# Affine weights of a modulated linear layer loaded in two transfers, and a one-column copy placed early on ScalarE

## The chip, the cores and the metric

The kernel runs on one core of one Trainium2 chip. The metric is the device time of one execution in microseconds (us), given as the median of several runs. A profiled execution gives the busy times, the waits and the transfers; its "span" runs from the first to the last instruction that the profiler saw.

## The reference, cut to what matters

The input x has 8 batches of 1024 tokens with 512 channels. A conditioned linear layer is computed first, and a mixture-of-experts feed-forward layer on its result; the sum with x is returned.

```python
styles = w @ (affine_w / 16).T + affine_b          # 8 x 512, w = cond_512 (8 x 256)
ws = weight[None] * styles[:, None, :]
dcoefs = rsqrt(sum(ws * ws, axis=2) + 1e-8)
y = einsum('blc,oc->blo', x * styles[:, None, :], weight) * dcoefs[:, None, :]
y = clip(y + bias, -256, 256)
...
x + shared_ffn(y) + routed_ffn(y)                  # 64 experts, 8 chosen per token
```

The change touches only what comes before the first products of the einsum: the loading of `affine_w`, the styles, and the scaling of x by them.

## The kernel before, in words

The 8192 tokens are handled as 16 tiles of 512. For about the first 241 us the conditioned layer is computed tile by tile (line L319), with the router's logits (L344); the shared experts follow (L124, L1083), up to about 1311 us, while the routing table is built; then the routed experts (L564, L584) run to the end. Every fp32 operand of a big product is split into a rounded high part and a remainder (`wh` and `wl` for the weights, `xh` and `xl` for the scaled tokens), and three products are summed for each: high by high, low by high, high by low.

The start of the kernel, which the change touches, goes like this. SyncE (SP) loads the affine weights `af` in one transfer of 512 KB (L225), then the four 256 KB row blocks of the linear layer's weights `wr` (L240). ScalarE (ACT) starts transfers too: the condition `cd` (L227), the vectors `vc` (L229, biases) and the four 256 KB blocks `xr` of the first token tile (L241), and only then computes. SP goes on with `rr`, `cs`, `ebb` (L243 to L245), eight stores of zeros (L293, L294) and the next token tile (L236).

`styles()` (L255 to L271) has TensorE multiply `af` by `cd` in 8 fp32 matmuls of 8 columns (L260; the profile counts each as two passes, 16 in all) into two PSUM tiles `ps`: the first holds the 128 channels of block 0, the second those of blocks 1 to 3. Then for each block k of 128 channels: ACT copies `wr` to `wh` (L262), VectorE (DVE) makes the styles `sty` of block 0, or of blocks 1 to 3, from `ps` (L266), ACT scales `xr` to `xh` (L302) and DVE makes `xl` (L303), DVE makes `wl` (L268; the profile shows the helper's line L72), and GpSimd (POOL) squares `wr` into `w2` (L271; the profile calls it `w`). TensorE multiplies by block k as soon as the parts are there (L319: per output block `xh` by `wh`, `xl` by `wh`, `xh` by `wl`). The squares are used later by the demodulation matmuls (L277, tile `psm`), which stand before block 3's products.

The order on PE, ACT and DVE is the one in which the calls are written (`manual_schedule`); the order on SP and POOL is the scheduler's. Each engine works off its list in order, so a waiting instruction holds up all behind it on its engine. The transfers that SP and ACT start share eight completion semaphores, taken in turn in the order of the code; a transfer isn't started before the one eight places ahead of it, which has the same semaphore, has landed. ScalarE needs a function table before its first computing instruction; the compiler puts the load of the table straight in front of it. Tiles of the pool `xa` that share a tag share two buffers: `af` and `wr` lie in those of `yf` (the layer's output), and the tag `lt` belongs to the router's logits.

Of the kernel before, what the change touches and what calls it, by code (L numbers as in the profile page):

```python
# [11 lines left out]
F32 = mybir.dt.float32  # L12
# [9 lines left out]
P = 128  # L22
B, L, C = 8, 1024, 512
# [43 lines left out]
def body(ctx, tc, xT, x, condT, wT, vecs, affT, rwT, ebias, wexp, shgu, shdn, cst, out):  # L67
    nc = tc.nc
    V, S, PE, GP, SP = nc.vector, nc.scalar, nc.tensor, nc.gpsimd, nc.sync

    def sub(o, a, b):
        V.tensor_tensor(o, a, b, ALU.subtract)  # L72
# [145 lines left out]
    with ExitStack() as actx:  # L218
        wa = actx.enter_context(tc.tile_pool(name="wa", bufs=1, reuse_waits="tile"))
        xa = actx.enter_context(tc.tile_pool(name="xa", bufs=2, reuse_waits="tile"))  # L220
        psa = actx.enter_context(tc.tile_pool(name="psa", bufs=1, space=PSUM, reuse_waits="tile"))

        xs, xhl, st = {}, {}, {}
        af = xa.tile([P, 2, C], F32, name="af", tag="yf")
        SP.dma_start(af, affT.rearrange("(k p) o -> p k o", p=P))  # L225
        cd = wa.tile([P, 2, B], F32, name="cd")
        S.dma_start(cd, condT.rearrange("(k p) b -> p k b", p=P))  # L227
        vc = wa.tile([P, 2, KC], F32, name="vc")
# [10 lines left out]
        for k in range(KC):  # L239
            SP.dma_start(wr[:, k], wv[k])  # L240
            S.dma_start(xs[0][k], xT[0, :, k * TT:(k + 1) * TT])  # L241
        rr = wa.tile([P, KC, E], F32, name="rr")
        SP.dma_start(rr, rwT.rearrange("(k p) e -> p k e", p=P))  # L243
        SP.dma_start(cs, cst)
# [10 lines left out]
        def styles():  # L255

            ps0 = [psa.tile([P, n, B], F32, name="ps0", tag="py", bufs=3) for n in (1, KC - 1)]
            for m in range(KC):
                for k in range(2):
                    PE.matmul(ps0[m > 0][:, max(m - 1, 0)], lhsT=af[:, k, m * P:(m + 1) * P], rhs=cd[:, k], start=k == 0, stop=k == 1)  # L260
            for k in range(KC):
                S.copy(wh[:, k], wr[:, k])  # L262
                if k < 2:
                    ks = slice(0, 1) if k == 0 else slice(1, KC)
                    n = ks.stop - ks.start
                    V.scalar_tensor_tensor(sty[:, ks], ps0[k], 1.0 / 16.0, vc[:, 1, ks].unsqueeze(2).to_broadcast([P, n, B]), ALU.mult, ALU.add)  # L266
                split_x(0, k)
                sub(wl[:, k], wr[:, k], wh[:, k].bitcast(F32))  # L268
                if k == 1:
                    V.tensor_tensor(sty2, sty, sty, ALU.mult)  # L270
                GP.tensor_tensor(w2[:, k], wr[:, k], wr[:, k], ALU.mult)  # L271
# [24 lines left out]
        def split_x(j, k):  # L296
            b = j * TT // L
            if k == 0:
                xhl[j] = ([], [])
            h = xa.tile([P, TT], F32R, name="xh", bufs=6)  # L300
            l = xa.tile([P, TT], F32R, name="xl", bufs=6)
            S.activation(h, xs[j][k], AF.Copy, scale=sty[:, k, b:b + 1])  # L302
            V.scalar_tensor_tensor(l, xs[j][k], sty[:, k, b:b + 1], h.bitcast(F32), ALU.mult, ALU.subtract)  # L303
            xhl[j][0].append(h)
            xhl[j][1].append(l)
# [111 lines left out]

        with tc.manual_schedule(engines={ET.PE, ET.Activation, ET.DVE}):
            styles()

            load_x(1)
# [823 lines left out]
```

## Time and profile before

| what | value |
|---|---|
| time, median of 3 runs | 3718.44 us (3717.13 to 3718.55) |
| the profiled execution's own time | 3718.36 us |
| its span | 3716.6 us |
| TensorE: busy, share of the span | 3684.8 us, 99% |
| VectorE, ScalarE, GpSimd busy | 2005.9, 1736.5, 2086.7 us |
| first TensorE instruction starts | 5.01 us |
| granted TensorE clock, mean | 0.996 |

Busy shares are means over the whole span. What a change at the start does must be read from the first 30 us: the timeline there (start, duration, engine, line, operation, tiles, count, and in brackets how long the engine was idle before and what ended that), the chain of waits followed back from the end, and the engine's busy time in chosen stretches with the clock that TensorE was granted and the rate of the transfers. "PEld" is TensorE's weight load, "SPq" and "ACTq" are transfers being started by SP and ACT.

### The profile page before, as it was taken

The page shows a single profiled execution, that of the slowest core. Times are in us where ns is not written, and L with a number is a line of the kernel's source. Part 1 is how long each engine was busy: PE and PEld are TensorE (multiplying, and loading weights), DVE is VectorE, ACT ScalarE, POOL GpSimd, SP SyncE. Part 2 cuts the span into 40 slices and gives each one's busy share as a digit, 9 for nine tenths or more (in the row PEclk, how much of TensorE's full clock was granted, in tenths as well). Part 3 has the DMA queues.
Part 4 walks back from the last instruction along what each step waited for, and adds up shares of the span by engine and source line. Part 5 has one row for each costly group of instructions (what it writes and reads, how often), then busy time and mean ns, then how long its engine had stood idle before and what let it go on. Part 6 is the DMA issues. An engine that isn't in the chain of part 4 may idle for free.

```text
span 3716.6 us, 49611 instructions
## 1 busy us (share of the span) xinstructions
PE 3684.8 (99%) x17819; PEld 3053.1 (82%) x17819; DVE 2005.9 (54%) x3196; ACT 1736.5 (47%) x2676; POOL 2086.7 (56%) x1597
## 2 busy tenths in 40 slices
PE   8999999999999999999999999999999999999997
PEld 7778888888888888888888888888888888888886
DVE  6766666666653255555455554555555555555553
ACT  6652111111111155555555555555555555555554
POOL 0001666666666055666666656666656666656563
PEclk9999999999999999999999999999999999999999
DMA  8862212122122277776777777788787777877664
GB/s 257 239 176 71 64 36 57 46 47 58 38 56 53 94 177 156 149 148 156 148 144 157 166 181 163 170 178 194 145 176 143 167 146 177 171 151 132 115 118 66
DMA packets 238739, 491.23 MB, mean 132 GB/s; under 512 B 43074, under 2 KB 75858, under 8 KB 230803
## 3 DMA queue, kind: packets, MB, share of 16 engines
q0 software_dynamic: 135840, 280.28, 40.6%
q1 hardware_dynamic: 101651, 206.63, 18.4%
q8 instruction: 142, 2.33, 0.3%
q14 instruction: 114, 0.93, 0.1%
q10 hardware_dynamic: 992, 1.06, 0.1%
HBM read 443.20 MB, written 195.63 MB: 172 GB/s over the span
## 4 chain that ended last, share of the span: by engine, by line
PE 98%; DVE 1%; DMA 0%; ACT 0%; issue 0%; POOL 0%; SPq 0%; ACTq 0%; DVEq 0%; POOLq 0%
PE pg L564 38%; PE po L584 20%; PE gu L124 19%; PE po L1083 9%; PE pt L541 4%; PE py L319 4%; PE pg L573 1%; PE plt L344 1%; DMA xr<-in_xT 0%; PE psm L367 0%; ACT yf L325 0%; DVE yl L72 0%; PE pg L578 0%; DVE yt L356 0%; PE ps L1004 0%
## 5 line engine op out<-in xcount | busy, mean ns | idle before, releaser
L591 POOL DMA_INDIRECT out<-oc,tokw x532 | 915.9, 1722 | 663.4 <-ACT oc L588 203.5
L1053 POOL DMA_INDIRECT tab_d<-tokw,ad x512 | 567.8, 1109 | 500.3 <-DVE h L136 220.1
L564 PE MATMUL pg<-xh,gh 128*128 128x512 f32 (+1 forms) x2176 | 838.7, 385 | 0.0
L564 PE MATMUL pg<-xh,gl 128*128 128x512 f32 (+1 forms) x2176 | 823.5, 378 | 0.0
L564 PE MATMUL pg<-xl,gh 128*128 128x512 f32 (+1 forms) x2176 | 821.6, 378 | 0.0
L537 POOL DMA_INDIRECT xg<-y_d,tokw x532 | 589.2, 1107 | 328.7 <-PE pt L541 141.5
L72 DVE TENSOR_TENSOR xl<-pt,xh 128x512 fp32r<-128x512 f32 x532 | 352.6, 687 | 406.6 <-ACT xh L544 405.7
L588 ACT ACTIVATE oc<-po,tokw 128x512 f32<-128x512 f32 x532 | 367.6, 691 | 316.4 <-PE po L584 279.6
L564 PEld LDWEIGHTS pg<-xh,gl 128*128 128x128 f32 x2176 | 409.1, 188 | 78.6
L564 PEld LDWEIGHTS pg<-xl,gh 128*128 128x128 f32 x2176 | 409.5, 188 | 71.8
L564 PEld LDWEIGHTS pg<-xh,gh 128*128 128x128 f32 x2176 | 408.7, 188 | 71.0
L584 PE MATMUL po<-dh,hh 128*128 128x512 f32 x1064 | 428.1, 402 | 0.8 <-ACT hh L713 0.8
L711 DVE TENSOR_TENSOR hf<-hf,pg 128x512 f32<-128x512 f32 x240 | 164.9, 687 | 488.0 <-PE pg L564 488.0
L584 PE MATMUL po<-dh,hl 128*128 128x512 f32 x1064 | 418.2, 393 | 0.0
L584 PE MATMUL po<-dl,hh 128*128 128x512 f32 x1064 | 415.3, 390 | 0.0
L72 DVE TENSOR_TENSOR gl<-wg,gh 128x1024 fp32r<-128x1024 f32 x312 | 376.2, 1222 | 52.0 <-ACT gh L552 51.4
L124 PE MATMUL gu<-yl,guh 128*128 128x512 f32 x1024 | 400.2, 391 | 0.0
L124 PE MATMUL gu<-yh,guh 128*128 128x512 f32 x1024 | 399.7, 390 | 0.0
L124 PE MATMUL gu<-yh,gul 128*128 128x512 f32 x1024 | 398.1, 389 | 0.0
L544 ACT CAST xh<-pt 128x512 fp32r<-128x512 f32 x532 | 296.9, 587 | 188.8 <-PE pt L541 133.1
L552 ACT CAST gh<-wg 128x1024 fp32r<-128x1024 f32 x312 | 323.9, 1048 | 27.1 <-PE pg L564 27.1
L708 ACT ACTIVATE hf<-pg 128x512 f32<-128x512 f32 x240 | 144.0, 600 | 294.3 <-PE pg L564 289.3
(246 smaller groups left out, 5206.5 us busy)
## 6 DMA issues: line engine op xcount, KB each, us to landing
wg<-in_wexp SPq DMA_DIRECT2D x156, 1024.0 KB
wd<-in_wexp SPq DMA_DIRECT2D x156, 512.0 KB
y_d<-yt SPq DMA_DIRECT2D x64, 256.0 KB
xn<-in_x SPq DMA_DIRECT2D x64, 256.0 KB
out<-xn SPq DMA_DIRECT2D x64, 256.0 KB
xr<-in_xT SPq DMA_DIRECT2D x60, 256.0 KB
yT_d<-yf SPq DMA_DIRECT2D x60, 256.0 KB
yr<-yT_d SPq DMA_DIRECT2D x60, 256.0 KB
```

The lines of the kernel that those rows point to most:

```text
L72: V.tensor_tensor(o, a, b, ALU.subtract)
L124: i_ = PE.matmul(p_, lhsT=w_[:, q * KC + k], rhs=y_[k], start=n == 0, stop=n == 3 * KC - 1)
L537: queued(GP.indirect_dma_start(xg[g % RXG].bitcast(F32), None, y_d, IOA(slot_tok[:, u.block + s:u.block + s + 1], 0)))
L544: S.copy(xh[u.xq][:, :, s * P:(s + 1) * P], pt_of(g).bitcast(F32))
L552: S.copy(a[u.q][:, sl], (wg, wg, wd)[c][u.kind][:, sl])
L564: PE.matmul(out, lhsT=w_[u.q][:, c:c + P], rhs=x_[u.xq][:, k, :w], start=n == 0, stop=n == 3 * KC - 1)
L584: PE.matmul(po[d % 2], lhsT=h_[u.q][:, k, s * P:(s + 1) * P], rhs=w_[u.q][:, k * C:(k + 1) * C], start=n == 0, stop=n == 5)
L588: S.mul(oc[d % ROC], po[d % 2], slot_w[:, u.block + s:u.block + s + 1])
L591: i_ = queued(GP.indirect_dma_start(out, IOA(slot_tok[:, u.block + s:u.block + s + 1], 0), oc[d % ROC], None, compute_op=ALU.add))
L711: mu = add((i, "mu", m), "DVE", 0.69, 0.15, t0, lambda b=b, f=f: V.tensor_tensor(hf[f % 3], hf[f % 3], pg[(b + 1) % 4], ALU.mult), si, p)
L1053: i_ = GP.indirect_dma_start(places, IOA(ad, 0), tw, None)
L1083: PE.matmul(acc[j][s], lhsT=h_[:, ts], rhs=w_[c], start=c == 0 and n == 0, stop=c == HC - 1 and n == 2)
```

## The change

The affine weights come in two transfers: `af[0]` with the first 128 channels (128 KB) stays first on SP, and `af[1]` with the other 384 (384 KB) is started behind the first block of `wr`. `af[0]` takes a buffer of the tag `lt`. A tile `nil` of one column is set to zero on DVE, and ACT copies it onto itself behind its third transfer (`cd`, `vc`, `xr` block 0), ahead of the other three blocks of `xr`; being ACT's first computing instruction, the copy now has the function table's load in front of it. The matmuls of `styles()` read `af[0]` for block 0 and `af[1]` for blocks 1 to 3.

```diff
@@ -221,8 +221,12 @@
         xs, xhl, st = {}, {}, {}
-        af = xa.tile([P, 2, C], F32, name="af", tag="yf")
-        SP.dma_start(af, affT.rearrange("(k p) o -> p k o", p=P))
+
+        nil = wa.tile([P, 1], F32, name="nil")
+        V.memset(nil, 0.0)
+        af = [xa.tile([P, 2, P], F32, name="af0", tag="lt"), xa.tile([P, 2, C - P], F32, name="af", tag="yf")]
+        afv = affT.rearrange("(k p) o -> p k o", p=P)
+        SP.dma_start(af[0], afv[:, :, :P])
         cd = wa.tile([P, 2, B], F32, name="cd")
@@ -239,6 +243,9 @@
         for k in range(KC):
             SP.dma_start(wr[:, k], wv[k])
             S.dma_start(xs[0][k], xT[0, :, k * TT:(k + 1) * TT])
+            if k == 0:
+                SP.dma_start(af[1], afv[:, :, P:])
+                S.copy(nil, nil)
@@ -257,7 +264,7 @@
             for m in range(KC):
                 for k in range(2):
-                    PE.matmul(ps0[m > 0][:, max(m - 1, 0)], lhsT=af[:, k, m * P:(m + 1) * P], rhs=cd[:, k], start=k == 0, stop=k == 1)
+                    PE.matmul(ps0[m > 0][:, max(m - 1, 0)], lhsT=af[m > 0][:, k, max(m - 1, 0) * P:max(m, 1) * P], rhs=cd[:, k], start=k == 0, stop=k == 1)
```

## The prediction

> **What bounds the kernel now.** The page comes first: it says which engine carries the span.
>
> ```profile
> span 3716.6 us, 49611 instructions
> PE 3684.8 (99%) x17819; PEld 3053.1 (82%) x17819; DVE 2005.9 (54%) x3196; ACT 1736.5 (47%) x2676; POOL 2086.7 (56%) x1597
> ```
>
> TensorE is idle for 31.8 us in all. The busy times by stretch (columns: stretch, length, busy time and instructions of PE, PEld, DVE, ACT, POOL, granted clock, transfer share, GB/s) tell where:
>
> ```profile
> 0.00:8.60 8.60, 3.59 (x17) 3.59 (x17) 1.68 (x4) 3.13 (x4) 4.24 (x12) 1.00 0.75 237
> 8.60:26.60 18.00, 18.00 (x81) 14.87 (x82) 11.09 (x21) 8.50 (x13) 2.93 (x2) 0.91 0.96 333
> ...
> 3700.00:3716.60 16.60, 0.00 (x0) 0.00 (x0) 0.00 (x0) 0.00 (x0) 2.48 (x2) 0.55 0.35 50
> ```
>
> 5.0 us go before TensorE's first instruction, 16.6 behind its last; in between it is nearly never idle, so a shift at the start goes through to the end. All that the change can move lies before 8.6 us. The chain of waits there:
>
> ```profile
> 0.75 4.21 DMA cd<-in_condT
> 4.97 0.04 issue
> 5.01 3.58 PE ps L260 x16
> 8.59 3.84 PE py L319 x9
> ```
>
> Transfers until 5.01, then the 16 passes of the styles, then the layer. The timeline of the same stretch shows that a second path ends at the same moment:
>
> ```profile
> 5.16 1.28 ACT L262 ACT_TABLE_LOAD   x1 [5.16 <-DMA af<-in_affT]
> 5.54 2.04 POOL L271 TENSOR_TENSOR w<-wr 128x512 f32<-128x512 f32 x2 [2.74 <-DMA wr<-in_wT]
> ...
> 6.45 0.62 ACT L262 CAST wh<-wr 128x512 fp32r<-128x512 f32 x1
> ...
> 7.30 0.72 ACT L302 ACTIVATE xh<-xr,sty 128x512 fp32r<-128x512 f32 x1 [0.23 <-DMA xr<-in_xT]
> ...
> 8.06 0.75 DVE L303 SCALAR_TENSOR_TENSOR xl<-xr,sty,xh 128x512 fp32r<-128x512 f32 x1 [1.82 <-ACT xh L302]
> ...
> 8.72 0.68 DVE L72 TENSOR_TENSOR wl<-wr,wh 128x512 fp32r<-128x512 f32 x1
> ...
> 9.46 0.29 PEld L319 LDWEIGHTS py<-xh,wl 128*128 128x128 f32 x1 [0.31 <-DVE wl L72]
> ...
> 10.46 2.93 POOL L271 TENSOR_TENSOR w<-wr 128x512 f32<-128x512 f32 x2 [2.88 <-DMA wr<-in_wT]
> ...
> 10.96 1.53 DVE L72 TENSOR_TENSOR wl<-wr,wh 128x512 fp32r<-128x512 f32 x1
> ...
> 12.41 1.02 DVE L270 TENSOR_TENSOR sty<-sty 128x32 f32<-128x32 f32 x1
> ```
>
> Two readings matter. First, `xh` started when block 0 of `xr` had landed (about 7.28), not because of the table load, which had been over since 6.44. Second, the layer's third matmul at 9.46 waited for `wl`. I call this moment T3; it is the later of two sums: end of the styles 8.59 + two matmuls of 0.43 (10.06 to 10.48 in the timeline) = 9.45, and end of `xh` 8.02 + 1.44 (`xl` and `wl`, to 9.46) = 9.46. Both paths are exactly as long, so the change gains only where it shortens both.
>
> **The change part by part.**
>
> *Styles, block 0 (4 passes).* They wait for `cd` and the first 128 KB instead of 512 KB. SP started its third `wr` transfer, which waits for `af`, at 4.99, and ACT its fourth `xr`, which waits for `cd`, at 4.79. So `cd` alone leaves 0.2 us to gain; with fewer bytes ahead it may land earlier, by 0.7 at most, I take 0.5. This makes the first 4 passes early, but not the other 12.
>
> *Styles, blocks 1 to 3 (12 passes, an added wait).* They wait for `af[1]`, and all of TensorE stands behind them. On SP `af[1]` now follows `wr` block 0, so it ends 768 KB into SP's order, where `wr` block 0 ends today; that landed at 5.54 (POOL starts its first square). Lower bound 5.5. Upper bound: blocks 0 and 1 of `xr` on ACT's queue, 512 KB, come in between; at the 358 GB/s of the stretch 4.5 to 6.0 that is 1.4 us more: 6.9. Block 1 is started later than now, so I take block 0 alone with little else, 6.1. The 12 passes take 12 x 0.224 (3.58 / 16) = 2.7, so the styles end at 8.8 (8.2 to 9.6), and this path gives T3 = 9.65 (9.1 to 10.5).
>
> *Table load and copy.* ACT's third transfer start ended at 2.26, so the load runs about 2.3 to 3.6 and the one-column copy costs at most the 0.17 us of the shortest DVE row here; its operand is set on DVE by 1.6 (a 0.48 us memset ends at 1.41). ACT was then idle waiting, so both are hidden. But the queue behind them shifts: block 1 of `xr` starts at about 3.9 instead of 2.3, block 2 behind the landing of `vc`, block 3 behind that of block 0 of `xr` (the built program shows these waits; today block 3 waits for `cd`, at 4.79). The `wh` copy stands behind block 3's start, so it now comes **after** `xr` block 0 has landed: landing + 0.34 (a start) + 0.62 (`wh`) + 0.72 (`xh`), less 0.09 of overlap = landing + 1.6, where today it is landing + 0.74. The 1.28 us that the load gives back were idle anyway; 0.85 are lost. In return `xr` block 0 lands earlier, because less lies ahead of it: at best by the 384 KB taken out of the front, 384 / 361 GB/s = 1.06 us (6.2), at worst not at all (7.3). I take 6.4, `xh` ends at 8.0, as now (7.8 to 8.9), and T3 by this path is 9.45 before the next term.
>
> *POOL's squares.* `wr` block 2 no longer waits for `af` (4.99), so SP starts it at about 2.7; blocks 1 and 2 land about 6.5 to 8.2 instead of up to 6.6 and 10.46. POOL's second and third squares (1.04 each) move from 6.6 and 10.46 to some time between 6.5 and 9.5, beside `xl` and `wl` of block 0. What that costs is in the rows: `wl` of block 1, started at 10.96 beside a square, took 1.53 instead of 0.68, and a product of 32 columns took 1.02, ending with the square at 13.4. Lower bound 0 (no square running at 8.7), upper bound 0.85 for `wl` and as much again for `xl`. I take 0.5 for both. T3 = 9.95, which is now the later path. Blocks 1's `wl` and the 32-column product come free in turn, but TensorE uses them only from 13.4 and 18.5 on: worth nothing.
>
> [...]
>
> [...]
>
> *The rest.* One transfer start more on SP (0.33 to 0.46 us) moves `wr` block 1 by so much. SP's later starts come earlier or stay: `rr` waits for `wr` block 0 instead of `xr` block 0 (7.23 now). They feed the second token tile, whose `xh` (18.89) is used from 26.6 on. The rest of the built program has the same order on every engine. The buffer in `lt` is free long before the logits need it. All this I set at 0.
>
> **Sum.** T3 goes from 9.46 to 9.95: +0.5 us. TensorE is then still at half clock: matmuls follow at 0.43 us until 11.77 and at 0.23 from 12.04 on. The clock column shows the same pair of paces later:
>
> ```profile
> 18.65:22.06 3.41, 3.41 (x34) 3.41 (x32) 2.02 (x3) 2.75 (x4) 0.00 (x0) 1.00 0.89 315
> 22.07:25.47 3.40, 3.40 (x10) 2.73 (x10) 2.06 (x8) 2.00 (x4) 0.00 (x0) 0.50 0.77 230
> ```
>
> If the step at 11.8 stays where it is, 0.5 us at half clock is 0.5 x 0.23 / 0.43 = 0.27 us in the end; if it moves along, 0.5. I take 0.3. The profiled execution would go from 3718.36 to 3718.7; the median of the runs is 0.08 above that execution, so the time is **3718.7 us**. The change's own bounds run from -0.4 (styles' lower bound, no collision) to +1.7 at T3.
>
> **The rivals.** *A small gain.* `xr` and `af[1]` land at their lower bounds and POOL is out of the way: T3 at 9.1 or a little less, 0.1 to 0.9 us gained: 3717.5 to 3718.4. For it: the first 128 KB are off the queue early. Against: both paths must shorten, and the `wh` copy now stands behind `xr`.
>
> *The clock decides, faster.* The step to full clock comes one stretch of 3.41 us earlier, or the half-clock stretch at 22.07 falls away because the demodulation sits otherwise in it: each is worth 3.41 x (1 - 0.54) = 1.6 us. 3715.9 to 3717.5. It needs TensorE's dense matmuls clearly before 8.4.
>
> *The clock decides, slower.* `af[1]` lands at 6.9 or a square holds up `wl` whole: T3 at 10.4 or later, the stretch 8.4 to 11.8 has too few dense matmuls, and half clock lasts 3.41 us longer: +1.6, and the delay itself up to +1.1: 3719.5 to 3721.2. [...] For it: the same trace was set to half clock after a stretch of only 8-column matmuls (18.65 to 22.06). Against: two thirds of the stretch would still be filled.
>
> *It doesn't do what it says* is half true already: the table load was not on the path; that is in the sum.
>
> **How the numbers follow.** Forecast (3718.4 to 3719.5) 0.50; small gain 0.20; clock faster 0.10; clock slower 0.15; something unseen 0.05. The range 3716.6 to 3720.8 takes in the forecast, the small gain and the nearer parts of both clock cases. 0.2% is 7.4 us, about what a measurement of this kernel can tell from no change, and no case above comes near it: only the unseen, 0.02 faster and 0.03 slower.
>
> **What would show it.** The table load at about 2.3 us; block 0's passes before 4.9 and a gap before the other twelve, with `af` as what ended it; `wh` behind the landing of `xr`; a DVE row of block 0 stretched beside a square; T3 between 9.5 and 10.4. Wrong: T3 below 9.1, no gap in the styles, or a difference that arises after 30 us, where I expect only a shift.

## The result, and the profile after

| what | before | after |
|---|---|---|
| time, median (lowest to highest) of 17 runs each | 3718.50 us (3714.80 to 3720.82) | 3724.88 us (3721.34 to 3728.49) |
| ratio of the times, 95% interval | | 1.0018 (1.0012 to 1.0024) |
| profiled execution, its span | 3718.36 us, 3716.6 us | 3724.88 us, 3723.1 us |
| T3, the layer's third matmul | 9.46 us | 13.08 us |

The change makes the kernel 6.4 us slower. That is less than the 7.4 us (0.2%) that the prediction took as the edge of "no change", but the interval lies clear of 1, the two sets of runs don't overlap, and the median is outside the predicted range.

The page of the changed kernel, its span and its busy times:

```profile
span 3723.1 us, 49614 instructions
PE 3686.5 (99%) x17819; PEld 3054.6 (82%) x17819; DVE 2006.6 (54%) x3197; ACT 1735.2 (47%) x2677; POOL 2074.9 (56%) x1597
```

TensorE does the same 17819 instructions and is busy 1.7 us more; the rest of the 6.5 us of span is idle time. The busy times by stretch of the changed kernel (columns as in the prediction) show where:

```profile
0.00:8.60 8.60, 1.24 (x5) 1.14 (x6) 1.15 (x4) 1.47 (x2) 3.24 (x11) 1.00 0.75 227
8.60:26.60 18.00, 17.34 (x83) 14.50 (x84) 10.14 (x15) 9.00 (x14) 3.48 (x3) 1.00 0.95 319
26.60:90.00 63.40, 61.11 (x254) 48.63 (x252) 48.33 (x91) 42.41 (x69) 0.00 (x0) 0.95 0.74 224
90.00:140.00 50.00, 44.12 (x185) 34.24 (x186) 37.84 (x102) 27.87 (x48) 0.77 (x1) 0.96 0.87 261
```

and the same view of the kernel before for the last two stretches:

```profile
26.60:90.00 63.40, 58.69 (x250) 46.03 (x249) 49.68 (x89) 42.48 (x69) 0.00 (x0) 0.98 0.77 235
90.00:140.00 50.00, 47.70 (x199) 37.85 (x198) 38.08 (x102) 30.06 (x50) 0.77 (x1) 0.93 0.87 268
```

Two things are to be seen. The start is worse than predicted: TensorE works 1.24 us of the first 8.6 instead of 3.59. And between 90 and 140 us, far from anything that the diff touches, TensorE is idle for 5.88 us instead of 2.30. How late each instruction comes, against the same instruction in the trace of before, joins the two. The table has it for VectorE (DVE) and for TensorE, worked out from both timelines by matching each engine's instructions in order:

| moment | T3 | 26 us | 90 us | 100 us | 140 us | 200 us | 241 us |
|---|---|---|---|---|---|---|---|
| VectorE later than before by, us | 3.6 | 3.0 | 3.2 | 3.7 | 5.4 | 6.8 | 6.5 |
| TensorE later than before by, us | 3.6 | 3.8 | 2.2 | 0.4 | 4.9 | 5.6 | 6.5 |

From 241 us on it stays between 6.4 and 6.5. By VectorE's row half of it arises before 26 us and half between 90 and 200. TensorE, which sets the time, shows another split: at 100 us it has made up for nearly all of the late start, and nearly all of the 6.4 us arises between 100 and 241. Two things in the stretches above go with that: it is idle for 2.29 us between 26.6 and 90 instead of 4.71, and its granted clock between 90 and 140 is 0.96 instead of 0.93. In all, from the start's step to full clock up to 241 us, both traces have 13.7 us at half clock.

**The start.** The timeline of the changed kernel (start, duration, engine, line, operation, count, and in brackets the idle time before and what ended it):

```profile
2.23 1.42 SPq L244 DMA_DIRECT2D wr<-in_wT  x3
2.29 1.28 ACT L248 ACT_TABLE_LOAD   x1 [2.29 <-issue]
...
3.42 1.02 PE L267 MATMUL ps<-cd,af 128*128 128x8 f32 x4 [3.42 <-DMA cd<-in_condT]
...
8.39 2.73 PE L267 MATMUL ps<-cd,af 128*128 128x8 f32 x12 [3.94 <-DMA af<-in_affT]
8.76 0.62 ACT L269 CAST wh<-wr 128x512 fp32r<-128x512 f32 x1 [4.99 <-DMA xr<-in_xT]
...
8.99 3.48 POOL L278 TENSOR_TENSOR w<-wr 128x512 f32<-128x512 f32 x3 [3.76 <-DMA wr<-in_wT]
9.29 0.72 ACT L309 ACTIVATE xh<-xr,sty 128x512 fp32r<-128x512 f32 x1
...
10.04 1.54 DVE L310 SCALAR_TENSOR_TENSOR xl<-xr,sty,xh 128x512 fp32r<-128x512 f32 x1 [5.39 <-ACT xh L309]
...
11.50 1.52 DVE L72 TENSOR_TENSOR wl<-wr,wh 128x512 fp32r<-128x512 f32 x1
...
13.08 0.79 PE L326 MATMUL py<-xh,wl 128*128 128x512 f32 x1 [0.66 <-DVE wl L72]
```

The table load is early, the first four passes are early, and then a gap of 3.94 us is ended by `af`. Block 0 of `xr` and `af[1]` both landed at about 8.35. `xl` and `wl` took 1.54 and 1.52 us beside POOL's squares (8.99 to 12.47) instead of 0.75 and 0.68.

**After 60 us.** What SyncE starts for one token tile, in the kernel before (count x4 stands for four transfers, the second number for the time that SP spent on the four starts):

```profile
63.47 2.81 SPq L359 DMA_DIRECT2D y_d<-yt  x4
66.33 3.48 SPq L334 DMA_DIRECT2D yT_d<-yf  x4
69.89 2.23 SPq L236 DMA_DIRECT2D xr<-in_xT  x4
```

and in the changed kernel:

```profile
66.70 3.43 SPq L366 DMA_DIRECT2D y_d<-yt  x4
70.17 4.12 SPq L341 DMA_DIRECT2D yT_d<-yf  x4
74.39 2.34 SPq L240 DMA_DIRECT2D xr<-in_xT  x4
```

The same eight stores take SP 7.69 us instead of 6.42, to the start of the token loads behind them. By the median over the loop, the third and the fourth store of `y_d` take 1.03 and 1.45 us instead of 0.63 and 1.24; the first two are unchanged. Measured from the first of the stores, the token loads start 0.9 to 1.6 us later in each of the eleven tiles that can be compared, 1.27 in this one. That reaches TensorE, as the chain of waits of the changed kernel shows in the stretch 90 to 140 us:

```profile
90.36 5.43 DMA xr<-in_xT
...
105.26 3.90 DMA xr<-in_xT
...
119.99 5.14 DMA xr<-in_xT
```

The chain runs from tile to tile through the landing of `xr`. In the kernel before it does so twice, at 54.71 and 69.89, and runs through `py` on TensorE for most of the stretch from 90 on:

```profile
54.71 5.57 DMA xr<-in_xT
69.89 5.86 DMA xr<-in_xT
...
95.01 5.60 PE py L319 x24
102.47 5.59 PE py L319 x24
108.50 5.57 PE py L319 x24
```

In the waits of 54 to 241 us, ACT's `xh` waited for `xr` 15.3 us before and 21.7 after.

None of these stores is in the diff. What the diff does to them is their source's address. The one-column tile `nil` is allocated in the first-stage pool ahead of everything else; it takes 32 bytes of each partition, and the tiles of that stage behind it move by 32 bytes. In the built program `yt`, `yf` and `xr` lay at 256 modulo 512 bytes before and lie at 288 after (the buffer for `af[0]` moves them 4096 bytes more, which changes nothing modulo 512). A `y_d` store reads `yt` in pieces of 512 bytes (the trace of before has 26580 packets of that size between 56 and 240 us, for 52 stores of 256 KB).

### The profile page after: what moved, and what is told of

The parts are those of the page before. It is cut to its first block, busy times and chain, and to the rows that moved or that the text cites. A ratio compares the mean times of both kernels' runs of the same rounds, so it can differ in the third digit from the quotient of the medians.

```text
span 3723.1 us, 49614 instructions
## 1 busy us (share of the span) xinstructions
PE 3686.5 (99%) x17819; PEld 3054.6 (82%) x17819; DVE 2006.6 (54%) x3197; ACT 1735.2 (47%) x2677; POOL 2074.9 (56%) x1597
## 4 chain that ended last, share of the span: by engine, by line
PE 96%; DVE 1%; DMA 1%; ACT 1%; issue 0%; POOL 0%; SPq 0%; ACTq 0%; DVEq 0%; POOLq 0%
PE pg L571 38%; PE po L591 20%; PE gu L124 19%; PE po L1090 9%; PE pt L548 4%; PE py L326 3%; PE pg L580 1%; DMA xr<-in_xT 1%; PE plt L351 0%; DVE xl L310 0%; ACT xh L309 0%; ACT yf L332 0%; DVE yl L72 0%; DVE yt L363 0%; DVE yf L333 0%
## 5 line engine op out<-in xcount | busy, mean ns | idle before, releaser
L544 POOL DMA_INDIRECT xg<-y_d,tokw x532 | 574.9, 1081 | 333.2 <-PE pt L548 145.9
```

The lines of the kernel that those rows point to most:

```text
L544: queued(GP.indirect_dma_start(xg[g % RXG].bitcast(F32), None, y_d, IOA(slot_tok[:, u.block + s:u.block + s + 1], 0)))
```

## The experiments

Three theories can explain the 6.4 us. The **address** theory: the 32 bytes lengthen the stores from `yt`, and that is most of it. The **rotation** theory: the extra transfer moves every later one to another of the eight completion semaphores. The **start** theory: T3 comes 3.6 us later, and the rest is the same delay passed on through the clock and the stalls. The expectations below call the first two A and R. Intervals are 95%; each kernel of an experiment ran 11 times, beside 32 or 33 runs of the kernel before on the same chip. T3 and the store starts come from one profiled execution of each kernel.

| kernel | `yt` modulo 512 | 3rd, 4th `y_d` start, us | T3 | time, us | ratio to before (interval) |
|---|---|---|---|---|---|
| before | 256 | 0.63, 1.24 | 9.46 | 3718.50 | |
| after | 288 | 1.03, 1.45 | 13.08 | 3724.88 | 1.0018 (1.0012 to 1.0024) |
| e1, column of 64 bytes | 320 | 1.01, 1.43 | 10.97 | 3723.30 | 1.0016 (1.0007 to 1.0025) |
| e2, shift alone | 288 | 1.03, 1.45 | 9.59 | 3723.48 | 1.0016 (1.0007 to 1.0025) |
| e3, split alone | 256 | 0.63, 1.24 | 11.44 | 3718.94 | 1.0003 (0.9994 to 1.0012) |
| e4, copy alone, 64 bytes | 320 | 1.01, 1.43 | 10.72 | 3721.90 | 1.0011 (1.0002 to 1.0020) |
| e5, change, old addresses | 256 | 0.64, 1.24 | 11.79 | 3719.62 | 1.0004 (0.9995 to 1.0013) |
| e6, shift of 128 bytes | 384 | 0.92, 1.24 | 9.95 | 3717.52 | 0.9998 (0.9988 to 1.0007) |
| e7, shift from the rows on | 288 | 1.03, 1.45 | 9.73 | 3724.36 | 1.0017 (1.0008 to 1.0026) |
| e8, shift behind the rows | 256 | 0.64, 1.24 | 9.35 | 3718.65 | 1.0001 (0.9992 to 1.0010) |
| e9, squares held | 256 | 0.64, 1.24 | 10.76 | 3719.49 | 1.0005 (0.9996 to 1.0014) |
| e10, parts adjacent | 256 | 0.64, 1.24 | 11.17 | 3719.10 | 1.0006 (0.9997 to 1.0015) |
| e11, start reordered | 256 | 0.63, 1.24 | 10.13 | 3718.20 | 1.0000 (0.9991 to 1.0009) |
| e12, addresses at 512 | 0 | 0.63, 1.25 | 9.32 | 3717.64 | 1.0001 (0.9992 to 1.0010) |

**e1, the column as wide as 64 bytes** (the rest of the change as it is):

```diff
-        nil = wa.tile([P, 1], F32, name="nil")
-        V.memset(nil, 0.0)
+        nil = wa.tile([P, 16], F32, name="nil")
+        V.memset(nil[:, :1], 0.0)
...
-                S.copy(nil, nil)
+                S.copy(nil[:, :1], nil[:, :1])
```

> The changed kernel, but the column tile is 16 columns wide (64 bytes a partition) and only its first column is set and copied; every later tile of the first stage then starts at a multiple of 64 bytes again, as before the change, and not at 32 beyond one. Theory A (address): about half of the loss arises after 90 us because the 32 byte shift makes SP's stores of the layer's rows drain more slowly; then the third and fourth row store of a tile take 0.63 and 1.24 us to start again instead of 1.03 and 1.45, and the time falls from 3724.9 to about 3721.5. Theory R (rotation): the extra transfer moves every later one to another semaphore of the eight; then nothing changes, 3724.9.

3723.30 us, and the stores as slow as with 32 bytes: a multiple of 64 does not help.

**e2, the shift without the change**: the kernel before with a column that nothing uses.

```diff
+        nil = wa.tile([P, 1], F32, name="nil")
+        V.memset(nil, 0.0)
         af = xa.tile([P, 2, C], F32, name="af", tag="yf")
```

> The kernel before with the one-column tile allocated and set to zero, no copy and no split: every later tile of the first stage starts 32 bytes further on, and the order of transfers is that of before. Theory A (address): the stores start as slowly as after the change and the time rises by about 3.5 to 3722. Theory R (rotation): same as before, 3718.5.

T3 is where it was (9.59), and yet the time is 3723.48 us, 5.4 more than the 3718.10 of the kernel before in that group. A shift of 32 bytes with no late start and no extra transfer gives nearly the whole loss. The rotation theory had 3718.5 here.

**e3, the split alone**: the change without `nil` and its copy, so the addresses stay.

```diff
-        nil = wa.tile([P, 1], F32, name="nil")
-        V.memset(nil, 0.0)
...
-                S.copy(nil, nil)
```

> The two transfers of the affine weights without the column tile and its copy; addresses are multiples of 64 bytes. Theory A: only the start is later, because the second part of the affine weights lands at about 8 us and the squares on POOL collide with block 0: third matmul of the layer at 11.5 to 13, time about 3721.5, and no loss after 90 us. Theory R: the extra transfer is there, so the loss after 90 us as well, 3724.

T3 is 2 us late (11.44: the second part of `af` is used from 7.86 on, the styles end at 10.59), and the time is 3718.94, no different from before by the interval, and less than either theory had said. The extra transfer is there and the loss isn't, so rotation is out; and a T3 of 11.44 costs far less than the 3 us that was expected of it.

**e4, the copy alone**, with a column of 64 bytes:

```diff
+        nil = wa.tile([P, 16], F32, name="nil")
+        V.memset(nil[:, :1], 0.0)
...
             S.dma_start(xs[0][k], xT[0, :, k * TT:(k + 1) * TT])
+            if k == 0:
+                S.copy(nil[:, :1], nil[:, :1])
```

> The copy behind ScalarE's third transfer without the split, the column tile 64 bytes wide. The table is loaded at 2.3 us, the copy of the first weight block stands behind the landing of the first token block: third matmul at about 10.3 instead of 9.46, worth 0.5 to 0.9 us: 3719.0 to 3719.4. Both theories say that nothing is lost after 90 us (no shift, no extra transfer). If the split alone makes the start late, the third matmul here is below 10.5; if the moved token transfers do, it is near 13.

3721.90 us, more than expected: the 64-byte column shifts the addresses as in e1, with e1's store starts, so this kernel tells little of the copy.

**e5, the whole change at the old addresses**: another tile of the same pool gets 8 columns (32 bytes) less.

```diff
-        ini = wa.tile([P, 256], I32, name="ini")
+        ini = wa.tile([P, 248], I32, name="ini")
```

> The whole change, with the scratch tile ini 8 columns (32 bytes) shorter, so that layer, row and token tiles lie as they did before the change, modulo 512 bytes; the column tile stays one column wide. Nothing of ini beyond column 208 is used. Theory A (address; e1's 64 bytes kept the slow stores, so the unit is larger than 64): row stores take 0.63 and 1.24 us to start, nothing is lost after 90 us, and what is left is the start, 0.5 to 2 us: 3719 to 3720.5. Theory R (the column's copy or the extra transfer itself): 3723.5 to 3725, stores 1.03 and 1.45.

3719.62 us, 5.3 less than the change itself, and 1.5 above the 3718.16 of before in its group, which the interval does not tell from 0. SP's starts for one tile are back, as the timeline of e5 shows:

```profile
65.02 2.86 SPq L366 DMA_DIRECT2D y_d<-yt  x4
67.92 3.76 SPq L341 DMA_DIRECT2D yT_d<-yf  x4
```

T3 is still at 11.79. Its delay against before is 2.35 us at 26 us and 1.08 at 90 on VectorE. On TensorE it is 3.3 us late at 30, 1.7 ahead at 100 and 2.5 late at 241. Its idle time between 90 and 140 is 4.65 us, which lies between the 2.30 of before and the 5.88 of the change: the stalls of one trace don't separate the theories here, the times do.

**e6, a shift of 128 bytes** in the kernel before:

```diff
+        nil = wa.tile([P, 32], F32, name="nil")
+        V.memset(nil[:, :1], 0.0)
```

> The kernel before with an unused tile of 128 bytes a partition in front, no copy, no split: everything in the first stage shifts by 128 bytes. If the address matters by a unit of 128 bytes, the time is that of before, 3718.2, and the stores 0.63 and 1.24; if by 256 or 512, about 3723.5 as with 32 bytes, and 1.03 and 1.45.

3717.52 us, no loss (by the interval at most 2.6 us). The stores are only partly as before: by the timeline of e6 the four of `y_d` take as long as in the changed kernel, but those of `yT_d` behind them do not:

```profile
63.35 3.43 SPq L361 DMA_DIRECT2D y_d<-yt  x4
66.83 3.44 SPq L336 DMA_DIRECT2D yT_d<-yf  x4
70.36 2.31 SPq L238 DMA_DIRECT2D xr<-in_xT  x4
```

**e7 and e8, which tile it is.** A pad of 32 bytes in the kernel before, once ahead of the `yt` buffers (e7) and once behind them (e8). In both, `yf`, `xr` and `wr` stay at 256 and the tiles behind `yt` (`xh` and the logits' buffer) move to 288; only `yt` differs, with the tiles `z` and `w2` that use its buffers at the start. In the built programs both have the same instructions in the same order.

```diff
+        pad = xa.tile([P, 1], F32, name="pad", bufs=1)
+        V.memset(pad, 0.0)
         w2 = xa.tile([P, KC, C], F32, name="w2", tag="yt")
```

> The kernel before with 32 bytes put in between the token tiles xr and the row tile yt: yt (whose stores go out as 512 byte pieces) and the split tiles behind it shift, the layer's output yf, xr and wr don't. Theory A1, yt's address alone counts: 3723.5 as with the shift of all. Theory A2, yf and xr count: 3718.2. Both in part: between.

> The control: the same 32 bytes put in behind yt, so that only xh, xl, the logits' tiles and the shared weights' first buffers shift, which hardly any transfer touches. Theory A (stores): same as before, 3718.2, stores 0.63 and 1.24. If an engine's operand address counted instead, 3722 or more.

e7 took 3724.36 us (3722.93 to 3725.32) and e8 3718.65 (3715.98 to 3720.70); the runs do not overlap. The timeline of e7:

```profile
63.89 3.42 SPq L361 DMA_DIRECT2D y_d<-yt  x4
67.35 3.98 SPq L336 DMA_DIRECT2D yT_d<-yf  x4
71.42 2.22 SPq L236 DMA_DIRECT2D xr<-in_xT  x4
```

and of e8:

```profile
63.76 2.81 SPq L361 DMA_DIRECT2D y_d<-yt  x4
66.62 3.47 SPq L336 DMA_DIRECT2D yT_d<-yf  x4
70.18 2.24 SPq L236 DMA_DIRECT2D xr<-in_xT  x4
```

In e7 the `yT_d` stores are slow too, though their source `yf` has not moved: they stand behind those of `yt`. The waits of e7 (total, times, longest):

```profile
ACT xh L304 <- DMA xr<-in_xT: 22.8, 9, 4.3
...
PEld py L321 <- ACT xh L304: 7.4, 5, 2.4
```

and of e8:

```profile
ACT xh L304 <- DMA xr<-in_xT: 15.9, 9, 2.9
...
PEld py L321 <- ACT xh L304: 3.6, 4, 1.8
```

The address of the `yt` buffers alone costs 6.2 us (3724.36 against 3718.16; by the interval 3 to 10). The clock isn't what differs: over the eleven runs the granted clock is 0.9965 in e7 and 0.9967 in e8, worth some 0.7 us (an estimate: 0.0002 of 3718 us). The way goes by the token loads: in the waits of 54 to 241 us over all fourteen traces, ACT's `xh` waited for `xr` 13.5 to 17.2 us where `yt` lies at 256 or 0, 17.5 to 22.8 at 288 or 320, and 17.7 at 384. e7's delay against before, on VectorE, grows late as in the changed kernel: 0.2 us at 26, 1.3 at 90, 3.8 at 140, 5.9 from 200 on.

**e9, the collision taken away**: e5 with POOL's squares of blocks 1 to 3 made to wait for `wl` of block 0.

```diff
-                sub(wl[:, k], wr[:, k], wh[:, k].bitcast(F32))
+                w_ = V.tensor_tensor(wl[:, k], wr[:, k], wh[:, k].bitcast(F32), ALU.subtract)
+                if k == 0:
+                    low = getattr(w_, "ins", w_)
...
-                GP.tensor_tensor(w2[:, k], wr[:, k], wr[:, k], ALU.mult)
+                g_ = GP.tensor_tensor(w2[:, k], wr[:, k], wr[:, k], ALU.mult)
+                if k:
+                    tc.add_manual_dep(getattr(g_, "ins", g_), low.name, ...)
```

> e5 (the change with the old addresses) with POOL's squares of blocks 1 to 3 made to wait for block 0's wl. If the collision on VectorE's and POOL's path is what stretches wl, wl takes 0.68 instead of 1.53 us and the third matmul comes 0.85 us earlier for the same landing of xr: end of xh + 1.44. The time falls by at most that, from 3719.6 to 3718.8 or stays within what can be told. If wl waited for something else, it stays at 1.5.

`wl` of block 0 in e9, and then in e5:

```profile
9.38 0.69 DVE L275 TENSOR_TENSOR wl<-wr,wh 128x512 fp32r<-128x512 f32 x1
```

```profile
10.20 1.53 DVE L72 TENSOR_TENSOR wl<-wr,wh 128x512 fp32r<-128x512 f32 x1
```

The collision is gone: `wl` takes 0.69 us. T3 comes 1.0 us earlier (10.76), but that is not all due to it. Block 0 of `xr` landed 0.9 us earlier in that trace, and T3 is now set by the styles, which end at 9.90 (7.17 + 2.73), plus two matmuls of 0.43. The time, 3719.49 us, does not change.

**e10, both parts of `af` next to each other** in SP's order, ahead of `wr` (e5 otherwise):

```diff
         SP.dma_start(af[0], afv[:, :, :P])
+        SP.dma_start(af[1], afv[:, :, P:])
...
-                SP.dma_start(af[1], afv[:, :, P:])
```

> e5 with the second part of the affine weights started right behind the first, ahead of the first weight block. My prediction's sum (bytes ahead at about 360 GB/s) would land it at about 5.0, as the whole af did before, and the styles end at 7.9 instead of 10.2. If the second part is late because ACT's token blocks and SP's weight blocks crowd it, not because of its place, it still lands at 6.5 or later. Time 3718.5 to 3719.6 either way.

The twelve passes of e10:

```profile
4.95 2.73 PE L267 MATMUL ps<-cd,af 128*128 128x8 f32 x12 [0.60 <-DMA af<-in_affT]
```

They start at 4.95 instead of 7.44 in e5, so the place of `af[1]` in SP's order counts for much of when it lands. But `xr` block 0 still landed only at about 7.1, `wl` took 1.52, and T3 is at 11.17. 3719.10 us.

**e11, a start put in the order of need**: e3 with the parts adjacent, `xr` block 0 ahead of `vc`, the last `wr` block last, and the squares held.

```diff
-        S.dma_start(vc, vecs)
+        SP.dma_start(af[1], afv[:, :, P:])
...
+        S.dma_start(xs[0][0], xT[0, :, :TT])
+        SP.dma_start(wr[:, 0], wv[0])
+        S.dma_start(vc, vecs)
```

> An attempt to beat both: affine weights in two adjacent transfers, no column and no copy, the first token block ahead of vc on ScalarE, the fourth token block ahead of the fourth weight block (so that its start waits for the affine weights and not for the first token block), squares 1 to 3 behind wl of block 0; old addresses. First 4 passes at 3.4, styles end near 7.9, xh near 7.5, third matmul at 8.8 to 9.0 instead of 9.46: 0.3 to 0.6 us less than before, 3717.7. If the first token block lands no earlier than 7.3, the third matmul stays at 9.4 and the time at 3718.2.

T3 is 10.13, still behind the 9.46 of before, and the time is that of before (3718.20 against 3717.72). Now `af[1]` is used only from 6.40 on, although it is started at 1.26 as in e10, so the styles give T3 no earlier than 9.99 (6.40 + 2.73 + 2 x 0.43). What ended last was ACT's path: without the copy the table load stands at 6.16, behind the start of the fourth `xr` block, and `wh`, `xh`, `xl` and `wl` follow each other from there to 10.07. Why `af[1]` is used 1.45 us later than in e10, no run shows.

**e12, addresses that are multiples of 512** in the kernel before:

```diff
-        cd = wa.tile([P, 2, B], F32, name="cd")
+        cd = xa.tile([P, 2, B], F32, name="cd", tag="lg")
...
-        ini = wa.tile([P, 256], I32, name="ini")
+        ini = wa.tile([P, 208], I32, name="ini")
```

> The kernel before with the scratch tile ini 48 columns shorter and cd in a buffer of the later logits tile, so that row, layer and token tiles start at multiples of 512 bytes instead of 256 beyond one. If only the place within 128 bytes counts, stores take 0.63 and 1.24 us as before and the time is 3718.2. If the crossing of a 512 byte line counts (the pieces of the row stores are 512 bytes long), the stores get faster still, 0.5 and 1.0, and up to 2 us go: 3716 to 3718.

3717.64 us and the same store starts as before: 256 modulo 512 was already as good as 0. No kernel tried beats the kernel before by more than the intervals.

## Why the prediction was wrong, point by point

**The step that failed is "The rest", "All this I set at 0".** It rests on "the rest of the built program has the same order on every engine". That is so, and it is not enough: I compared the order of the instructions and never the addresses of the tiles. I saw the one-column tile only as a DVE memset and an ACT copy. As an allocation it moves `yt` from 256 to 288 modulo 512, and that is worth 5.4 (e2) to 6.2 us (e7) of the 6.4. The prediction named the sign of its own error: "a difference that arises after 30 us, where I expect only a shift". On TensorE nearly all of the delay in the changed kernel arises there. Its premise that TensorE "is nearly never idle" in between passed over 7.0 us of stalls between 26.6 and 140 us in the kernel before (4.71 and 2.30), part of them behind token loads: later loads had a place to cost.

**The two landings were mis-sized.** `af[1]` was taken at 6.1 with 6.9 as the upper end, block 0 of `xr` at 6.4 with 7.3; both came at about 8.35. That is one trace: over the kernels that start `af[1]` in this place (e1, e3, e5, e9, after) `af[1]` came between 6.9 and 8.4, so its upper end was too low, and block 0 of `xr` between 6.6 and 8.4, in e1 and e9 within its range. I counted the bytes ahead of each transfer in its own queue and a part of the other queue. What is started behind them may count too: `wr` blocks 1 to 3, which no longer wait for `af`, are started at 2.23 to 3.65 and move alongside. The prediction used that earlier start for POOL's squares and not for the landings. But no run holds these three back alone, so this cause isn't shown. The place in the order is: 4.95 for `af[1]` in e10.

**The sum for T3 held in form.** With the measured terms the prediction's own formula gives it: end of `xh` 10.01, plus 1.44 for `xl` and `wl`, plus the collision of 1.63 (0.79 and 0.84) is 13.08. Predicted were 8.0 + 1.44 + 0.5. So 2.0 of the 3.1 us are the landing, and 1.1 the collision, which came near its upper bound for both instructions. The prediction's own bound of +1.7 at T3 had room for only one of the two (7.3 + 1.6 + 1.44 + 0.85 = 11.19); with both it would have been +2.6. "Landing + 1.6" for the end of `xh` was right (8.35 to 10.01). That a square of 1.04 us holds `wl` up whole, as the slower clock rival allowed, no run shows: beside squares `wl` of block 0 took 1.52 us in the changed kernel, e1 and e10 and 1.53 in e5, 0.84 to 0.85 more than before.

**What a late T3 costs was about right in size, not in its way.** With the addresses put back, T3 at 10.8 to 11.8 costs 0.8 to 1.8 us in the medians of e3, e5, e9 and e10, none of them clear of 0. The rival "the clock decides, slower" had put T3 at 10.4 or later at 3719.5 to 3721.2; e5 took 3719.62, and e3, e9 and e10 came out just below, at 3718.94 to 3719.49. But half clock did not last the whole stretch of 3.41 us longer that this rival needs: full clock, where the pace of the matmuls goes from 0.43 to 0.23 us, began 3.3 us behind T3 in the changed kernel (at 16.35) and 4.5 behind it in e5 (at 16.32), against 2.4 (11.82) before. Nor is it a mere shift: in e5's trace the delay turns into a lead by 100 us and comes back, and the prediction had weighed only the clock at the start, not the stalls after 26 us. How the 1.5 us of e5 come about stays open. The shift alone (5.4 us in e2, 6.2 in e7) and the change without it (1.5 in e5) add up to 6.9 to 7.7 us; 6.4 were measured, which is within their intervals.

**Right:** the table load at 2.3 us, the early four passes and the gap ended by `af`, `wh` behind the landing of `xr`, DVE rows stretched beside a square, and that the load of the table was not on the path, before or after. The four passes came even earlier than allowed, by 1.6 us instead of 0.7 at most, and it gained nothing.

**The packets.** The traces show the address in the stores' packets as well: the mean of the 512-byte packets between 56 and 240 us is 32.3 ns in before, e5 and e8 (`yt` at 256 modulo 512) and in e12 (at 0), 34.7 to 35.5 with a shift of 32 or 64 bytes (288 and 320), and 36.6 with 128 (384). The length of the packets alone does not give the time: e6, with the longest, loses nothing (3717.52 us).

**Open:** why the third and the fourth store take SP longer to start with a shift of 32 or 64 bytes (1.03 and 1.45, 1.01 and 1.43 us) than with 128 (0.92 and 1.24). The runs show the address, the stores, the loads behind them and the time, and not what lies between the address and the start. Nor is it settled why e6 loses nothing: its token loads start 0.5 to 1.2 us later than before, but its trace has 6.8 us at half clock in the layer, against 13.7 before, and that may hide a small loss.

## What to carry to other kernels

A new tile, however small, is also a shift of every tile that is allocated behind it (here by 32 bytes for one column): compare the tiles' addresses in the two built programs, as well as the order, and keep the sources of stores that are read in short pieces where they were (here, with pieces of 512 bytes, 256 modulo 512; a shift of 32 cost 5.4 to 6.2 us). The bytes ahead of a transfer did not give its landing: both landings here came about 2 us later than that count, and differed by 1.5 to 1.7 us between the changed kernel and e1, which start them in the same order. Where a loss arises long after the edit, look for the instructions there whose duration changed, and move one tile at a time.

## What the runs showed of the hardware that was not expected

- The address of a store's source in SBUF changed the time that SP needs to start it: with 512-byte pieces the third and fourth of four stores took 1.03 and 1.45 us at 288 modulo 512, 0.63 and 1.24 at 256 or 0, 1.01 and 1.43 at 320, 0.92 and 1.24 at 384.
- Slow stores slowed the starts behind them on the same queue: those of `yT_d` took 0.93 us in the mean over the loop in e7 against 0.75 in e8 (the slowest 24 of them 1.48 against 1.11), with the same address of their own source.
- Starting `af[1]` 0.5 us earlier (at 1.26 instead of 1.76, one place ahead in SP's order) made it land 2.5 us earlier: it was used from 4.95 us on in e10 and from 7.44 on in e5. One trace each: in e11, with the same start but other transfers moved too, it was used from 6.40 on.
- A delay at the start need not last: TensorE was 3.3 us late at 30 us in e5 and 1.7 ahead at 100. It was idle for 2.87 us between 26.6 and 90 instead of 4.71, and was granted full clock from 86.92 to 93.74 where the kernel before was granted 0.50. At 241 us it was 2.5 late again.
